# Four cross-attention layers on one core: pieces put ahead of a pair's scores, and the maxima subtracted one pair before the exponentials

## The chip, the core and the metric

The kernel runs on one core of one Trainium2 chip, in float32. Five engines work side by side, each through its own instructions in order: TensorE (PE in the profile; PEld is its weight load), VectorE (DVE), ScalarE (ACT), GpSimd (POOL), and SyncE (SP), which issues the DMAs. The metric is the device time of one execution in microseconds. Over three runs the kernel before took 4752.23 us (median; 4741.26 to 4752.79).

## The reference

`x` is [1, 2048, 256], the context [1, 1601, 512]. Four layers follow each other, each adding its output to `x`. Layers 0, 2 and 3 are "masked": 16 heads of 64, and a bias on four of the 1601 keys. Layer 1 is "grouped": an RMS norm, 16 heads of 16, four key heads, no mask.

```python
q = hidden_states @ Wq;  k = encoder_hidden_states @ Wk;  v = encoder_hidden_states @ Wv
logits = jnp.einsum('bhqd,bhkd->bhqk', q, k) * scale + col_bias
probs = jax.nn.softmax(logits, axis=-1)
out = jnp.einsum('bhqk,bhkd->bhqd', probs, v) @ Wo + bo + residual
```

## The kernel before

**Units and steps.** A masked layer is cut into 8 blocks of two heads (class `Masked`, L423) and 4 groups of 512 queries; one block with one group is a *unit* (class `Unit`, L682). The three masked layers have 96 units, the grouped one 16. A unit has 13 *steps*, one per 128 keys (the last has 65). The main loop (L1266) issues two steps at a time, a *pair*. Three phases of different units are in flight in a pair: at step t the scores of the unit with number t // 13, the exponentials of 18 steps back (NT + DELAY), and the values of 20 steps back (LAG 2, so the values of a pair use the exponentials of the pair before).

**One step of a masked unit.** `masked_scores` (L707): matmuls of keys with queries for both heads into a PSUM tile `s` [128, 2, 512] (L713), a ScalarE copy of `s` into an SBUF tile `p` (L725), and a VectorE maximum of `s` into the running `top` (L728, L730; none in step 0). `maxima` (L766), after the last step: eight transposes of `top` into another `s` tile (L773), a VectorE reduction to `ntop` (L774), and two DMAs that spread the row maxima over all partitions into `spread`. `maxima_spread` (L796): a ScalarE copy of `spread` into the PSUM tile `b` (L799). `subtract` (L802): `p <- p + b` on VectorE (L804). `masked_exp` (L806): the exponential in place on ScalarE (L809), and the running sum on GpSimd (L812, L814). `values` (L834): matmuls of `p` with `v` into `po` (L849); after the last step a copy to `oT` (L871).

**Pieces.** All other TensorE work is cut into pieces, which `Pieces` (L1069) hands out, at most one large one to a pair. *Fill pieces* (the list `fill`) are the key and value projections of the next block: `kT` (L459, copied by ScalarE in L460) and `v` (L413, L417), 14 for the four units of a block. *Due pieces* have a step of their own (`due`): the next unit's `queries` (L483, copied in L486) at step 11, `denominators` (transposes of `sums` in L887, reduction in L891) at step 8, `divide` (GpSimd, L912) and `project` (L920, added to `xs` in L932) at step 3. `own` runs what is due, `pair` adds a fill piece where nothing large was due. Fill pieces and queries write the PSUM tile `pm`, of which there is one. `denominators`, `project` and `maxima` write an `s` tile. **There are two `s` tiles** (pool `ps_s`, bufs=2), shared by these three and the scores; each covers two PSUM banks. Below these three are called *tile pieces* (the class argument `shared=False` marks the first two).

**Order.** TensorE, ScalarE and VectorE execute exactly in the order in which the Python code issues (the loop at L1321 chains each instruction to the one before on its engine). SyncE and GpSimd are ordered by the framework. In a pair of masked steps the order before is: subtract 0 and 1; scores 0 and 1 (matmuls, copy, maximum of each); exponentials 0 and 1; the copy of `spread`, where the next pair begins a unit; values 0 and 1; the pieces; `maxima`, where a unit's scores ended. So VectorE runs: subtract, subtract, maximum, maximum, and then whatever the piece leaves to it. ScalarE runs: copy, copy, exponential, exponential, and then the piece's copy.

Where a unit's values end in the first step of a pair (`ends`), its last values stand before the exponentials and the new unit's first values after the pieces.

The 22 `p` tiles (NP) are taken at the copy of the scores and come free when values and sum of the step are done, 20 steps later.

Of the kernel before, what the change touches and what calls it, by code (L numbers as in the profile page):

```python
# [32 lines left out]

@with_exitstack
def tile_cross_attention_stack(ctx: ExitStack, tc: tile.TileContext, t: dict, out: bass.AP):

# [29 lines left out]
    x, cond = t["x"], t["ctx_2048"]  # L68
# [8 lines left out]
    NT = len(TCH)  # L77
# [23 lines left out]
    class Scores:  # L101
# [16 lines left out]
        def pair(self, shape=(2, QB)):  # L118
            return self.pairs.tile([P, *shape], FP, name="s")
# [50 lines left out]
    def key_order(tok):  # L170
# [27 lines left out]
        first = const.tile([P, NTOK], FP, name="first")  # L198
        keep = small.tile([P, NTOK], FP, name="keep", bufs=1)
        nc.vector.tensor_tensor(pair, across(tok), along(tok), ALU.is_equal)  # L200
        nc.vector.tensor_tensor(pair, pair, before, ALU.mult)
        nc.vector.tensor_reduce(first, pair, AX.X, ALU.max)
        nc.vector.tensor_scalar(first, first, 0.0, None, ALU.is_equal)
        nc.vector.scalar_tensor_tensor(first, tok, 0.0, first, ALU.is_ge, ALU.mult)
# [18 lines left out]
        def sources(a, b):  # L223
            n = b - a
            wide = [P, n, NTOK]

            def tokens_of(v):
                return v.rearrange("p (o j) -> p o j", o=1).to_broadcast(wide)

            def at_positions(v):  # L230
                return v.rearrange("p (n o) -> p n o", o=1).to_broadcast(wide)

            test = probs.tile(wide, FP, name="p")
            spec = probs.tile([P, n], FP, name="p")
            place = probs.tile([P, n], FP, name="p")
            to, at = src[:, a:b], pos[:, a:b]
            nc.vector.tensor_tensor(test, at_positions(at), tokens_of(where), ALU.is_ge)
            nc.vector.tensor_reduce(to, test, AX.X, ALU.add)
            nc.vector.tensor_tensor(to, to, at, ALU.add)

            nc.vector.tensor_scalar(place, at, count, float(T), ALU.add, ALU.subtract)
            nc.vector.scalar_tensor_tensor(to, place, 0.0, to, ALU.is_lt, ALU.mult)
            nc.vector.tensor_tensor(test, at_positions(place), tokens_of(rank), ALU.is_equal)
            nc.vector.tensor_tensor(test, test, tokens_of(mine), ALU.mult)
            nc.vector.tensor_reduce(spec, test, AX.X, ALU.add)
            nc.vector.tensor_tensor(to, to, spec, ALU.add)
# [435 lines left out]
    class Unit:  # L682
# [119 lines left out]
        def subtract(self, c):  # L802
            m = TCH[c][1]
            nc.vector.tensor_tensor(self.p[c][:m], self.p[c][:m], self.less[:m], ALU.add)  # L804
# [205 lines left out]
    units = []  # L1010
# [4 lines left out]
    of = {}  # L1015
# [36 lines left out]
    def first_unit(i):  # L1052

        if i < NT / 2:
            first_block(i)
        if i == 1:
            layers[0].load_wo(made[0, 0])
            for b in range(NB):
                keep(0, b)
                pieces.at(2 * i + 2 + 2 * b, [(0, biases[b])])  # L1060
        if i == 3:
            token_marks(0)
        if i == 7:
            small_constants()
            for l in range(1, NL):
                token_marks(l)
            start_block(0)

    class Pieces:  # L1069
# [4 lines left out]
        def __init__(self):  # L1074
            self.fill, self.later = deque(), deque()
            self.due = {}
            self.credit = 0.0

        def at(self, step, found):
            for steps, piece in found:  # L1080
                self.due.setdefault(step + steps, []).append(piece)

        def own(self, steps):

            cost, taken = 0.0, False
            for step in steps:
                for piece in self.due.pop(step, ()):
                    piece.run()
                    cost += piece.cost
                    taken |= piece.shared and piece.cost > 0  # L1090
            return cost, taken

        def pair(self, steps, pairs):

            cost, taken = self.own(steps)
            many = len(self.fill) + len(self.later) > pairs
            while self.fill and not taken and (many or not cost):
                piece = self.fill.popleft()
                piece.run()
                cost += piece.cost  # L1100
                taken = piece.shared and piece.cost > 0

        def steps(self, steps, share):


            self.credit = max(min(self.credit + share, 2.5), -2.5)
            cost, taken = self.own(steps)
            self.credit -= cost
            while self.fill and not taken and self.credit >= self.fill[0].cost / 2:
                piece = self.fill.popleft()  # L1110
                piece.run()
                self.credit -= piece.cost
                taken = piece.shared and piece.cost > 0
# [13 lines left out]
    pieces = Pieces()  # L1127
# [53 lines left out]
    DELAY, LAG = 5, 2  # L1181
# [81 lines left out]
    def masked(unit):  # L1263
        return unit and unit.masked

    for first in range(0, N + NT + DELAY + LAG + 16, 2):  # L1266
        pair = [Step(first), Step(first + 1)]

        if any(masked(x.scoring) for x in pair):
            if psum.banks:  # L1270
                psum.by_pairs()
        elif pair[0].exping and not pair[0].exping.masked and not psum.banks:
            psum.singly()

        kn, cn = divmod(first + 2 - NT - DELAY, NT)
        ahead = of[kn] if cn == 0 and 0 <= kn < len(units) and of[kn].masked else None
        three = not ahead and not any(masked(x.exping) for x in pair)
        for x in pair:
            x.begin()
        for x in pair:  # L1280
            if masked(x.exping):
                if x.cb == 0 and x is pair[1]:
                    x.exping.maxima_spread()
                x.exping.subtract(x.cb)
        for x in pair:
            if masked(x.scoring):
                x.scoring.masked_scores(x.ca)

        ends = all(masked(x.valuing) for x in pair) and pair[0].cv == NT - 1
        if ends:  # L1290
            pair[0].valuing.values(NT - 1)
        for x in pair:
            if masked(x.exping):
                x.exping.masked_exp(x.cb)
        if ahead:
            ahead.maxima_spread()
        if not ends:
            for x in pair:
                if masked(x.valuing):
                    x.valuing.values(x.cv)  # L1300
        first_unit(first // 2)
        together = masked(pair[0].scoring) and (masked(pair[1].exping) or not pair[1].exping)
        for x in pair:
            x.grouped(three)
            x.end()
            if not together:
                pieces.steps([x.step], x.share())
        if together:
            pieces.pair([first, first + 1], round(pair[0].units_left() * NT / 2))
        if ends:  # L1310
            pair[1].valuing.values(0)
        for x in pair:
            if x.scoring and x.ca == NT - 1:
                x.scoring.maxima()
                if not x.scoring.masked:
                    pieces.at(first + 2, [(0, Piece(x.scoring.maxima_rows, 0.3))])


    last = {}
# [39 lines left out]
```

## Time and profile before

| | |
|---|---|
| median of three runs | 4752.23 us (4741.26 to 4752.79) |
| the profiled execution, its own time | 4745.24 us |
| its span, first to last instruction | 4743.5 us |
| TensorE busy | 4596.3 us, 97% |
| VectorE busy | 3744.2 us, 79% |
| ScalarE busy | 3226.5 us, 68% |
| GpSimd busy | 2977.4 us, 63% |
| mean granted TensorE clock | 0.992 |
| mean DMA traffic | 71 GB/s |

Busy time is per engine; a busy TensorE is one with matmuls in its pipeline, not one at its peak. An idle time stands with the instruction that followed it, and with what that instruction had waited for (the releaser). The chain of waits follows the end of the program back from releaser to releaser. L713 is line 713 of the kernel before. All times in what follows are in microseconds (us) from the start of the span, unless they are durations.

### The profile page before, as it was taken

The page shows a single profiled execution, that of the slowest core. Times are in us where ns is not written, and L with a number is a line of the kernel's source. Part 1 is how long each engine was busy: PE and PEld are TensorE (multiplying, and loading weights), DVE is VectorE, ACT ScalarE, POOL GpSimd, SP SyncE. Part 2 cuts the span into 40 slices and gives each one's busy share as a digit, 9 for nine tenths or more (in the row PEclk, how much of TensorE's full clock was granted, in tenths as well). Part 3 has the DMA queues.
Part 4 walks back from the last instruction along what each step waited for, and adds up shares of the span by engine and source line. Part 5 has one row for each costly group of instructions (what it writes and reads, how often), then busy time and mean ns, then how long its engine had stood idle before and what let it go on. Part 6 is the DMA issues. An engine that isn't in the chain of part 4 may idle for free.

```text
span 4743.5 us, 64047 instructions
## 1 busy us (share of the span) xinstructions
PE 4596.3 (97%) x23943; PEld 1914.1 (40%) x23943; DVE 3744.2 (79%) x3768; ACT 3226.5 (68%) x4013; POOL 2977.4 (63%) x1436
## 2 busy tenths in 40 slices
PE   8999999999989999999999999999999999999998
PEld 5444444444433333343444444344444444444433
DVE  5888888888876666653788888888888888888887
ACT  4777777777635555555677777777777777777776
POOL 3777777778730000000677777777777777777787
PEclk9999999999989999999999999999999999999999
DMA  4322323222201010021232232222232223232211
GB/s 150 85 84 79 88 77 86 81 80 78 74 27 38 20 29 21 20 61 39 79 89 84 78 89 78 84 80 82 76 91 73 86 81 85 75 86 77 84 36 39
DMA packets 349892, 337.63 MB, mean 71 GB/s; under 512 B 116421, under 2 KB 305381, under 8 KB 349580
## 3 DMA queue, kind: packets, MB, share of 16 engines
q1 hardware_dynamic: 346310, 328.14, 24.6%
q8 instruction: 189, 3.10, 0.3%
q0 software_dynamic: 1152, 3.28, 0.2%
q10 hardware_dynamic: 2118, 2.10, 0.1%
q14 instruction: 123, 1.01, 0.1%
HBM read 318.49 MB, written 14.69 MB: 70 GB/s over the span
## 4 chain that ended last, share of the span: by engine, by line
PE 87%; DVE 10%; issue 1%; ACT 1%; POOL 0%; DMA 0%; another core or an unknown queue 0%; ACTq 0%; DVEq 0%; POOLq 0%
PE po L849 28%; PE s L713 20%; PE t L744 9%; PE pm L413 7%; PE pm L459 6%; PE pm L483 4%; PE s L920 4%; DVE rden L891 2%; PE s L887 2%; DVE ntop L774 2%; DVE xs L932 2%; PE s L773 2%; DVE top L730 1%; DVE p L804 1%; PE t L819 1%
## 5 line engine op out<-in xcount | busy, mean ns | idle before, releaser
L814 POOL TENSOR_TENSOR sums<-sums,p 128x1024 f32<-128x1024 f32 x1145 | 2711.0, 2368 | 736.8 <-ACT p L809 566.0
L725 ACT COPY p<-s 128x1024 f32<-128x1024 f32 (+1 forms) x1248 | 1234.2, 1014 | 655.3 <-PE s L713 567.6
L804 DVE TENSOR_TENSOR p<-p,b 128x1024 f32<-128x1024 f32 (+1 forms) x1248 | 1461.2, 1210 | 55.5 <-ACT b L799 54.4
L849 PE MATMUL po<-p,v 128*64 128x512 f32 (+3 forms) x8320 | 1493.5, 522 | 4.9 <-ACT p L809 2.6
L730 DVE TENSOR_TENSOR top<-s,top 128x1024 f32<-128x1024 f32 (+1 forms) x1056 | 1291.4, 1223 | 234.1 <-ACT p L725 171.3
L713 PE MATMUL s<-q,kT 64*128 64x512 f32 (+1 forms) x4992 | 1336.7, 629 | 85.9 <-DVE ntop L774 23.2
L809 ACT ACTIVATE p<-p 128x1024 f32<-128x1024 f32 (+1 forms) x1248 | 1254.7, 1057 | 43.8 <-DVE p L804 42.6
L849 PEld LDWEIGHTS po<-p,v 128*64 128x64 f32 (+3 forms) x8320 | 365.7, 125 | 1115.8 <-issue 889.3
L713 PEld LDWEIGHTS s<-q,kT 64*128 64x128 f32 (+1 forms) x4992 | 388.6, 181 | 722.7 <-issue 215.5
L831 ACT ACTIVATE p<-t 128x512 f32<-128x512 f32 (+1 forms) x760 | 413.8, 594 | 297.6 <-PE t L819 256.5
L757 DVE TENSOR_REDUCE row_top<-t 128x1 f32<-128x512 f32 x700 | 451.2, 686 | 196.8 <-PE t L819 165.2
L912 POOL TENSOR_TENSOR oT<-oT,by 128x512 f32<-128x512 f32 x111 | 141.6, 1276 | 656.4 <-DMA by<-cols 336.1
L819 PE MATMUL t<-q,kT 32*128 32x512 f32 (+1 forms) x1520 | 489.1, 643 | 0.0
L744 PE MATMUL t<-kT,q 32*128 32x512 f32 (+1 forms) x1880 | 481.9, 553 | 0.0
L413 PEld LDWEIGHTS pm<-wv,ct 128*128 128x128 f32 (+1 forms) x2600 | 300.4, 187 | 130.4 <-issue 69.0
L413 PE MATMUL pm<-wv,ct 128*128 128x128 f32 (+2 forms) x2600 | 333.3, 281 | 1.7 <-ACT vs L417 0.7
L459 PE MATMUL pm<-ct,wk 128*128 128x256 f32 (+1 forms) x1344 | 316.7, 379 | 5.4 <-ACT ct L284 4.3
L774 DVE TENSOR_REDUCE ntop<-s 128x8 f32<-128x1024 f32 x96 | 117.6, 1225 | 228.4 <-PE s L773 228.4
L459 PEld LDWEIGHTS pm<-ct,wk 128*128 128x128 f32 x1344 | 232.2, 191 | 161.1 <-issue 99.3
L744 PEld LDWEIGHTS t<-kT,q 32*128 32x128 f32 x1880 | 182.5, 185 | 163.1 <-issue 96.7
L799 ACT COPY b<-spread 128x1024 f32<-128x1024 f32 x96 | 97.5, 1015 | 150.9 <-DVE p L804 150.0
L920 PE MATMUL s<-oT,wo 128*128 128x512 f32 x376 | 187.4, 621 | 2.8 <-DVE row_top L757 1.7
(176 smaller groups left out, 2249.8 us busy)
## 6 DMA issues: line engine op xcount, KB each, us to landing
ct<-ctxT SPq DMA_DIRECT2D x288, 512.0 KB
xT<-xT SPq DMA_DIRECT2D x100, 512.0 KB
spread<-cols SPq DMA_DIRECT2D x96, 512.0 KB
by<-cols SPq DMA_DIRECT2D x190, 128.0 KB
xT<-xs SPq DMA_DIRECT2D x16, 512.0 KB
ct<-ctxT SPq DMA_DIRECT2D x48, 130.0 KB
wk<-in_L_xattn_Wk_dram SPq DMA_DIRECT2D x24, 256.0 KB
wv<-in_L_xattn_Wv_dram SPq DMA_DIRECT2D x24, 256.0 KB
```

Of the source, the lines that this page charges most:

```text
L413: nc.tensor.matmul(pv[:md, d, :f], ct(k)[:, d * P : d * P + md], wv[:, k, :], start=(k == 0), stop=(k == NCT - 1),)
L459: nc.tensor.matmul(pk, u.wk[:, k, :], ct(k), start=(k == 0), stop=(k == NCT - 1))
L713: nc.tensor.matmul(s[:m, h, :], self.u.kT[r, a : a + m], self.q[r, :], start=True, stop=(a != TAIL),)
L725: nc.scalar.copy(p[:m], s[:m])
L730: nc.vector.tensor_tensor(self.top[:m], s[:m], self.top[:m], ALU.max)
L744: nc.tensor.matmul(s[:, at : at + n], self.q[r, ts(q, P)], self.u.kT[r, a : a + n], start=True, stop=True,)
L757: nc.vector.tensor_reduce(self.top[:, of, q, k : k + 1], s, AX.X, ALU.max)
L804: nc.vector.tensor_tensor(self.p[c][:m], self.p[c][:m], self.less[:m], ALU.add)
L809: nc.scalar.activation(p[:m], p[:m], AF.Exp)
L814: nc.gpsimd.tensor_tensor(self.sums[:m], self.sums[:m], p[:m], ALU.add)
L819: nc.tensor.matmul(s[:m], self.u.kT[r, a : a + m], self.q[r, :], start=True, stop=True)
L849: nc.tensor.matmul(to, v, p, start=(c == 0 and not part), stop=(c == NT - 1 and part != 0))
```

## The change

Three things move in pairs of masked steps; no computation is added or taken away.

1. *Pieces in front.* A new flag `pieces.scored` is set when a pair issued a tile piece. In the pair after that one (`front`), `pieces.pair` runs before the scores instead of at the end. If it ran something large, the end of that pair gets no piece.
2. *Subtractions one pair ahead.* The two subtractions that feed a pair's exponentials are issued in the pair before: that of its first step after the values and before the piece at the end, that of its second step as the very last thing, after `maxima`. The copy of `spread` goes with the first subtraction of a unit.
3. *Exponentials around the scores.* The first exponential of a pair is issued before its scores (behind the piece in front, if any), the second after them.

VectorE's order in a pair becomes: maximum, maximum, first subtraction for the next pair, what the piece at the end leaves to it, second subtraction. ScalarE's: the front piece's copy, exponential 0, copy, copy, exponential 1, the end piece's copy.

```diff
         def own(self, steps):
             cost, taken = 0.0, False
-            for step in steps:
-                for piece in self.due.pop(step, ()):
+            for step in sorted(step for step in self.due if step <= max(steps)):
+                for piece in self.due.pop(step):
                     piece.run()
                     cost += piece.cost
+                    self.scored |= piece.cost > 0 and not piece.shared
                     taken |= piece.shared and piece.cost > 0
             return cost, taken
...
+    def subtract(unit, c):
+        if c == 0:
+            unit.maxima_spread()
+        unit.subtract(c)
...
-        kn, cn = divmod(first + 2 - NT - DELAY, NT)
-        ahead = of[kn] if cn == 0 and 0 <= kn < len(units) and of[kn].masked else None
-        three = not ahead and not any(masked(x.exping) for x in pair)
+        ahead = []
+        for step in (first + 2, first + 3):
+            kn, cn = divmod(step - NT - DELAY, NT)
+            unit = of[kn] if 0 <= kn < len(units) else None
+            ahead.append((unit, cn) if masked(unit) else None)
+        three = not any(ahead) and not any(masked(x.exping) for x in pair)
         for x in pair:
             x.begin()
-        for x in pair:
-            if masked(x.exping):
-                if x.cb == 0 and x is pair[1]:
-                    x.exping.maxima_spread()
-                x.exping.subtract(x.cb)
+
+        together = masked(pair[0].scoring) and (masked(pair[1].exping) or not pair[1].exping)
+        steps, left = [first, first + 1], 0
+        if together:
+            left = round(pair[0].units_left() * NT / 2)
+        front = pieces.scored
+        pieces.scored = False
+        taken = pieces.pair(steps, left) if together and front else 0.0
+        if masked(pair[0].exping):
+            pair[0].exping.masked_exp(pair[0].cb)
         for x in pair:
             if masked(x.scoring):
                 x.scoring.masked_scores(x.ca)
...
-        for x in pair:
-            if masked(x.exping):
-                x.exping.masked_exp(x.cb)
-        if ahead:
-            ahead.maxima_spread()
+        if masked(pair[1].exping):
+            pair[1].exping.masked_exp(pair[1].cb)
         if not ends:
             for x in pair:
                 if masked(x.valuing):
                     x.valuing.values(x.cv)
         first_unit(first // 2)
-        together = masked(pair[0].scoring) and (masked(pair[1].exping) or not pair[1].exping)
+        if ahead[0]:
+            subtract(*ahead[0])
...
-        if together:
-            pieces.pair([first, first + 1], round(pair[0].units_left() * NT / 2))
+        if together and not taken:
+            pieces.pair(steps, left)
         if ends:
             pair[1].valuing.values(0)
         for x in pair:
             if x.scoring and x.ca == NT - 1:
                 x.scoring.maxima()
+                pieces.scored |= x.scoring.masked
...
+        if ahead[1]:
+            subtract(*ahead[1])
```

More of the change, by code (lines that the diff above doesn't have):

```diff
@@ L1077, in __init__ @@
             self.credit = 0.0
+            self.scored = False
         def at(self, step, found):
@@ L1101, in pair @@
                 taken = piece.shared and piece.cost > 0
+            return cost
         def steps(self, steps, share):
```

## The prediction

> **What bounds the kernel now.** I read the page's busy times and its chain by engine first.
>
> ```profile
> PE 4596.3 (97%) x23943; PEld 1914.1 (40%) x23943; DVE 3744.2 (79%) x3768; ACT 3226.5 (68%) x4013; POOL 2977.4 (63%) x1436
> ...
> PE 87%; DVE 10%; issue 1%; ACT 1%; POOL 0%; DMA 0%; another core or an unknown queue 0%; ACTq 0%; DVEq 0%; POOLq 0%
> ```
>
> TensorE sets the end, save for 10% of the chain that lies on VectorE. Where that is, the chain of waits in the middle of the last layers shows (start, us, what):
>
> ```profile
> 3043.80 1.93 PE s L920 x4
> 3045.73 0.02 issue
> 3045.75 1.24 DVE xs L932
> 3046.99 0.04 issue
> 3047.03 1.13 PE s L713 x4
> 3048.16 1.87 PE po L849 x8
> 3050.03 1.92 PE pm L459 x8
> 3051.95 1.92 PE s L713 x8
> 3053.87 1.87 PE po L849 x8
> ```
>
> After a tile piece (here `project`) one of the two `s` tiles is full. The second scores of the next pair wait for VectorE to empty it. From the end of the piece to the start of the values it takes 48.16 - 45.73 = 2.43, where an undisturbed pair takes 1.92: 0.51 lost. The waits by releaser name three kinds of such tiles, near 96 times each:
>
> ```profile
> PEld s L713 <- DVE ntop L774: 99.7, 93, 1.1
> PEld s L713 <- DVE rden L891: 98.2, 91, 1.1
> PEld s L713 <- DVE xs L932: 87.9, 81, 1.1
> ```
>
> Two units are 13 pairs, a cycle; busy times for one (span, PE, PEld, DVE, ACT, POOL):
>
> ```profile
> 3019.50:3097.30 77.80, 76.26 (x343) 32.40 (x341) 65.89 (x59) 56.75 (x66) 61.22 (x28) 1.00 0.29 82
> ```
>
> A cycle has six tile pieces: 6 x 0.51 = 3.06 of its 77.8 is all that putting pieces in front can win. VectorE is 85% busy here. Last, one undisturbed pair in the timeline:
>
> ```profile
> 3015.29 2.34 DVE L804 TENSOR_TENSOR p<-p,b 128x1024 f32<-128x1024 f32 x2
> 3015.70 1.99 PE L713 MATMUL s<-q,kT 64*128 64x512 f32 x8
> ...
> 3016.93 1.93 ACT L725 COPY p<-s 128x1024 f32<-128x1024 f32 x2 [1.30 <-PE s L713]
> 3017.62 1.94 PE L849 MATMUL po<-p,v 128*64 128x512 f32 x8
> 3017.98 2.56 DVE L730 TENSOR_TENSOR top<-s,top 128x1024 f32<-128x1024 f32 x2 [0.35 <-ACT p L725]
> ...
> 3018.74 2.02 ACT L809 ACTIVATE p<-p 128x1024 f32<-128x1024 f32 x2
> ```
>
> The maximum does not start with its scores: it starts 0.04 after the *copy* of the same tile (3016.93 + 1.01). The subtractions run before the scores are there, so nothing waits for them.
>
> **What the skill says.** The Trainium skill, "PSUM — Partial Sum Buffer", section "PSUM bank collisions raise a hardware error": the compiler's scheduler puts a dependency between any two instructions on different engines that touch the same bank, two readers too. The trace agrees: the 0.35 idle above; so I hold copy, then maximum, for an order that the change can't loosen. "Perfetto Trace Analysis", section "Tensor Engine Instruction (MATMUL, LD_WEIGHTS)": VectorE and ScalarE are strict FIFO, and TensorE's end times are modelled. The former is what the code's chained order shows; for the latter I take distances in the chain, not TensorE's busy time. The same page's "Optimization Strategy" reads a gap that repeats as a sign of too few buffers; here 0.26 of idle in front of L713, and two `s` tiles.
>
> **The change, part by part.** *Pieces in front.* After a tile piece, a piece of 1.92 covers VectorE's 1.24: the 0.51 goes. What is late next: nothing follows the pair's values, so the next pair's scores come at once. *Subtractions.* The same 26 per cycle, moved from ahead of the maxima to behind them. The spread copies keep their place on ScalarE almost to the instruction. *Exponential 0* moves ahead of the copies. This makes a ring that was not there before: maxima of a pair, subtraction 0 for the next pair, exponential 0, copy 0, maximum 0 and 1 of that pair. Queued behind the waiting exponential on ScalarE are both copies; for them waits VectorE's maximum, and for this the `s` tile that the next tile piece needs.
>
> Steps, from back-to-back rows: maxima 1.22 + 1.33 (2.55); from their start to the next operation 2.46; a subtraction ends 1.21 after its start; exponential 1.05; the copy behind it 0.93; kT copy 0.37; hand-over 0.04. The ring: (2.46 + 1.21 - 2.55 = 1.13) + 0.04 + 1.05 + 0.93 + 0.04 + 2.55 = 5.74 a pair. TensorE's pair with one piece is 1.92 + 1.87 + 1.92 = 5.71. So the ring is no shorter than TensorE's own work, and what it once loses it doesn't win back.
>
> Follow a front pair C and the next, D, from the end of C's front piece (0):
>
> - ScalarE: kT copy 0.04 to 0.41, exponential 0 to 1.4, copy 0 to 2.34 (its scores were ready at 1.13).
> - VectorE: maxima of C 2.38 to 4.93; subtraction 0 for D to 6.05.
> - TensorE: scores and values of C to 3.79; D's first scores to 4.75; the second must wait for the second maximum, 4.98, and with refilling the array (the group after an idle takes 1.13, not 0.96) end at 6.04; values of D to 7.91. Lost so far 0.33.
> - ScalarE: exponential 0 of D 6.09 to 7.15, copy 0 to 8.08 (its scores lay ready at 4.95). VectorE: maximum 0 of D 8.12 to 9.34.
> - If D ends in a tile piece, it needs the tile of D's first scores: it starts at 9.39 instead of 7.91, with refilling 1.63 lost.
>
> If D ends in a fill piece, it runs 7.91 to 9.83 and hides this lag, but the lag stays: pair E's maximum 0 ends at 9.34 + 5.74 = 15.08, its values at 9.83 + 3.79 = 13.62, and E's tile piece loses 1.51 + 0.15 = 1.66.
>
> Over a cycle, numbering pairs from 0 at the start of a unit that begins a pair, tile pieces end pairs 1 (project), 4 (denominators), 6 (maxima), 8, 10, 12 (maxima), and fronts are 0, 2, 5, 7, 9, 11. Losses: behind each front 6 x 0.33 = 1.98; pairs 1, 8 and 10 at 1.63 = 4.89; pair 4 1.66; pair 12, where the queries run first and the transposes need the second maximum (10.67 against 9.83), 0.89 + 0.15 = 1.04; pair 6 none, since a fill piece precedes its transposes. Sum 9.57, less the 3.06 that is saved: **+6.5 per cycle**.
>
> Scores and masked exponentials overlap in 30.6 units of layer 0 (13 x 32 - 18 steps) and 62.6 of layers 2 and 3: 46.6 cycles. The last two have no fill pieces (a cycle there takes 74.0 already, VectorE 65.9); the ring alone is 13 x 5.74 = 74.6 and six reductions that push subtraction 1 make some +3 each. 44.6 x 6.5 + 2 x 3 = 296. The profiled execution's own 4745 plus 296 is 5041; that execution lay 7 below the median shown, so I say **5045**.
>
> At nothing I put: the wider `due` search (issue order only). DMAs: queries in front free their buffer, and so issue the next xT load, some 3.8 earlier, fill pieces the next context load likewise; both are prefetches. `denominators` and `maxima` issue their small DMAs on SP later by their stall, up to 1.7; `divide` comes three steps later and `project` eight, some 8 and 23 away, the spread two pairs; that slack hides it, and without it a late spread would hold subtraction 0 and so the ring, one for one. GpSimd (61 of 78) follows the exponentials. The grouped layer (PE 868 of 880) keeps its order but for the 18 steps at each border.
>
> **Unknown sizes.** Not shown is how the ring's members overlap when they alternate across engines. With isolated means (1.21 + 1.06 + 1.01 + 2 x 1.22, four hand-overs) it is 5.87, and each tile piece, two rings on, loses up to 0.2 more: +8.5 per cycle, 5141. With every step 3% shorter it is 5.57: some 0.25 less per event, +5, 4978.
>
> **Rivals.**
> 1. *The maximum needs no copy* (faster). Were maximum 0 of D free to follow its scores, VectorE would run maxima and subtractions alone, 4.7 a pair (5.9 with a reduction), finish maximum 0 of D near 7.15, and the tile piece at 7.58 would find its tile free: all of 3.06 won, 44.6 x 3.06 = 136, 4609. It decides at 1.45 of the 1.96 lost per event: less lost than 0.51, and the change gains. For it: the maxima's values need only `s`. Against it: 0.35 behind the copy, 203 such idles in the trace of `top`. 9%.
> 2. *The wait only changes place*: tile pieces lose about the 0.51 that scores lose now. 4745 within 14. It wants a ring shorter by 1.45; the rows leave no such room. 3%.
> 3. *The lag is partly caught up*: steps 0 have no maximum (1.2 of relief per unit), and stalls of TensorE let the ring gain. At a quarter to a third of the losses kept beyond the gain, +1 to +3 per cycle: 4790 to 4880. 8%.
> 4. *Also the `p` tiles run short*: copies already wait 42.9 for sums on GpSimd (34 times). Later exponentials make later sums; three times that on top of the upper bound is beyond 5140. 5%.
>
> That the change doesn't take effect I rule out: the flag is set by every tile piece.
>
> **How the numbers follow.** Forecast 75%, then 9, 3, 8, 5. The range 4870 to 5140 holds most of the forecast and the top of the third rival. About 0.3% (14) is what a measurement can tell from no change. Faster 0.10, same 0.03, slower 0.87.
>
> **What would show it.** Right: the waits of L713 for ntop, rden and xs fall to a fraction, and TensorE's idle before `project` and `denominators` grows to 1 to 1.5 each, released by the maximum of `top`; ScalarE idles 1 to 2 before exponential 0, released by the subtraction (now 42.6 in all, then several hundred); a cycle takes 83 to 86; VectorE's and ScalarE's shares of the chain rise at TensorE's cost. Wrong: a cycle under 77, maxima that start while the copy of their tile runs, or tile pieces that start right behind the values.

## The result

The change made the kernel slower: 4953.85 us against 4752.51 (medians of four runs each), a ratio of 1.0429 with a 95% interval of 1.0411 to 1.0447. The forecast was 5045 with a range of 4870 to 5140. So the sign was right, and the loss is two thirds of what was worked out: 205.6 us in the profiled executions (spans 4949.1 and 4743.5) instead of some 300.

The page of the changed kernel, busy times and the chain by engine:

```profile
PE 4562.2 (92%) x23943; PEld 1919.9 (39%) x23943; DVE 3754.8 (76%) x3768; ACT 3186.8 (64%) x4013; POOL 2981.9 (60%) x1436
...
PE 60%; DVE 17%; ACT 13%; issue 7%; DMA 1%; POOL 1%; ACTq 0%; DVEq 0%; SPq 0%; POOLq 0%
```

The chain has moved from TensorE (87% before) to a round trip: 17% on VectorE, 13% on ScalarE, which had 1%, and 7% in which the engine waited for nothing that the profile shows ("issue"). The shares alone don't tell a loss: with pieces in front alone, which is faster than the kernel before, the three engines have 63%, 23% and 7%. The waits by releaser (total, times, longest; lines are two further down than before, so L715 are the scores, L732 the maximum, L727 the copy, L806 the subtraction, L811 the exponential, L922 `project`, L889 `denominators`):

```profile
ACT p L811 <- DVE p L806: 590.8, 347, 8.9
DVE top L732 <- ACT p L727: 507.3, 484, 9.4
...
PE s L922 <- DVE top L732: 124.6, 88, 1.5
...
PE s L889 <- DVE top L732: 100.5, 89, 1.5
```

ScalarE's wait for the subtractions is 590.8 where it was 42.6, and the two tile pieces wait 1.4 and 1.1 us each for a maximum, a wait that the kernel before did not have. What was to go is mostly gone. Call *eviction* the VectorE operation that empties the tile of a tile piece: `xs` for `project`, `ntop` for `maxima`, `rden` for `denominators`. The waits of the scores' weight loads for `xs` and `ntop` were 87.9 and 99.7, and are 9.4 and 6.1. That for `rden` fell only from 98.2 to 70.0; where the matmuls themselves wait for it, as at 3014.64 in the timeline (0.39), the front piece was the short one of 65 keys, which takes 0.93 and not 1.8.

One turn of the new ring, in the timeline behind a front pair (start, us, what, and in brackets the idle before it):

```profile
3004.06 2.55 DVE L732 TENSOR_TENSOR top<-s,top 128x1024 f32<-128x1024 f32 x2 [0.66 <-ACT p L727]
...
3005.48 2.32 PE L715 MATMUL s<-q,kT 64*128 64x512 f32 x8
...
3006.53 2.34 DVE L806 TENSOR_TENSOR p<-p,b 128x1024 f32<-128x1024 f32 x2
3007.73 1.94 PE L851 MATMUL po<-p,v 128*64 128x512 f32 x8
3007.78 1.06 ACT L811 ACTIVATE p<-p 128x1024 f32<-128x1024 f32 x1 [1.40 <-DVE p L806]
3008.74 1.91 ACT L727 COPY p<-s 128x1024 f32<-128x1024 f32 x2
...
3009.77 2.55 DVE L732 TENSOR_TENSOR top<-s,top 128x1024 f32<-128x1024 f32 x2 [0.89 <-ACT p L727]
```

From maxima to maxima it takes 3009.77 - 3004.06 = 5.71. The scores that the copy at 3008.74 reads had started at 3005.48. The next thing on TensorE is `denominators`, at 3011.14, after 1.47 of idle: it needed the tile of the first maximum, which ended at about 3011.0.

A cycle of 13 pairs, from one `denominators` to the same place 13 pairs on:

```profile
3011.14:3093.17 82.03, 75.32 (x365) 33.53 (x365) 66.11 (x59) 55.73 (x66) 61.34 (x29) 1.00 0.29 79
```

82.03 against 77.8: +4.2 a cycle. Over the 44.6 cycles with fill pieces this is 189 of the 205.6 us; the last two, without fill pieces, take 77.84 and 77.85 instead of 75.34 and 73.78 (from `rden` to `rden`), 6.6 more. The prediction had named 83 to 86 for a cycle as a sign that it is right; that sign did not come, 82.0 lies below it.

### The profile page after: what moved, and what is told of

It is laid out like the page before. It is cut to its first block, busy times and chain, and to the rows that moved or that the text cites. A ratio compares the mean times of both kernels' runs of the same rounds, so it can differ in the third digit from the quotient of the medians.

```text
span 4949.1 us, 64074 instructions
## 1 busy us (share of the span) xinstructions
PE 4562.2 (92%) x23943; PEld 1919.9 (39%) x23943; DVE 3754.8 (76%) x3768; ACT 3186.8 (64%) x4013; POOL 2981.9 (60%) x1436
## 4 chain that ended last, share of the span: by engine, by line
PE 60%; DVE 17%; ACT 13%; issue 7%; DMA 1%; POOL 1%; ACTq 0%; DVEq 0%; SPq 0%; POOLq 0%
PE s L715 16%; PE po L851 13%; DVE top L732 13%; ACT p L727 10%; PE t L746 8%; PE pm L415 5%; PE pm L461 4%; PE s L922 4%; ACT p L811 2%; PE s L775 2%; PE pm L485 2%; DVE p L806 1%; PE s L889 1%; DVE rden L893 1%; DVE top L730 1%
## 5 line engine op out<-in xcount | busy, mean ns | idle before, releaser
L732 DVE TENSOR_TENSOR top<-s,top 128x1024 f32<-128x1024 f32 (+1 forms) x1056 | 1292.4, 1224 | 563.1 <-ACT p L727 507.3
L811 ACT ACTIVATE p<-p 128x1024 f32<-128x1024 f32 (+1 forms) x1248 | 1326.4, 1063 | 592.6 <-DVE p L806 590.8
L806 DVE TENSOR_TENSOR p<-p,b 128x1024 f32<-128x1024 f32 (+1 forms) x1248 | 1479.2, 1208 | 19.5 <-ACT b L801 18.4
L715 PE MATMUL s<-q,kT 64*128 64x512 f32 (+1 forms) x4992 | 1311.8, 627 | 42.0 <-DVE rden L893 18.0
L727 ACT COPY p<-s 128x1024 f32<-128x1024 f32 (+1 forms) x1248 | 1197.0, 1007 | 53.8 <-PE s L715 50.6
L715 PEld LDWEIGHTS s<-q,kT 64*128 64x128 f32 (+1 forms) x4992 | 399.6, 182 | 780.9 <-DVE top L732 348.0
L461 PE MATMUL pm<-ct,wk 128*128 128x256 f32 (+1 forms) x1344 | 305.6, 371 | 3.5 <-issue 2.8
L922 PE MATMUL s<-oT,wo 128*128 128x512 f32 x376 | 186.2, 618 | 130.0 <-DVE top L732 124.6
L730 DVE TENSOR_TENSOR top<-s,p 128x1024 f32<-128x1024 f32 x96 | 117.5, 1224 | 210.9 <-ACT p L727 210.8
L419 ACT COPY v<-pm 128x256 f32<-128x256 f32 (+1 forms) x168 | 60.1, 357 | 241.3 <-PE pm L415 239.5
```

The costliest lines, as they stand in the source:

```text
L461: nc.tensor.matmul(pk, u.wk[:, k, :], ct(k), start=(k == 0), stop=(k == NCT - 1))
L715: nc.tensor.matmul(s[:m, h, :], self.u.kT[r, a : a + m], self.q[r, :], start=True, stop=(a != TAIL),)
L727: nc.scalar.copy(p[:m], s[:m])
L732: nc.vector.tensor_tensor(self.top[:m], s[:m], self.top[:m], ALU.max)
L811: nc.scalar.activation(p[:m], p[:m], AF.Exp)
```

## Experiments

The change has three parts: F, pieces in front; S, the subtractions a pair ahead; E, exponential 0 ahead of the score copies (which needs S). The theory on record is that of the ring (subtraction 0, exponential 0, copy 0, maxima). Rivals lay the loss on F or on S alone. The first four runs take the parts singly and two at a time; the kernel before that ran beside them took 4748.61. Each ratio is to the kernel before that ran beside it, with its 95% interval; it can differ by some 0.1% from the quotient of the medians.

### F and S without E

```diff
-        if masked(pair[0].exping):
-            pair[0].exping.masked_exp(pair[0].cb)
         for x in pair:
             if masked(x.scoring):
                 x.scoring.masked_scores(x.ca)
...
+        if masked(pair[0].exping):
+            pair[0].exping.masked_exp(pair[0].cb)
         if masked(pair[1].exping):
             pair[1].exping.masked_exp(pair[1].cb)
```

> The change, with exponential 0 issued behind the two score copies again (pieces in front and early subtractions stay). Ring theory (subtraction 0, exponential 0, copy 0, maximum 0 and 1, each waiting for the last, is what costs): with the exponential behind the copies the copies follow their scores, the ring is open, and the 0.5 us behind each tile piece is won at least in part: 4690 to 4745, no idle of TensorE in front of project and denominators. Rival A (pieces in front cost: the pair behind a front pair comes too early for two s tiles): the front pieces are all still there, so 4880 or more. Rival B (the new place of the subtractions on VectorE costs): likewise 4880 or more.

Measured: 4680.32 us, ratio 0.9856 (0.9836 to 0.9876), **faster than both kernels**, and better than expected. Moving one exponential per pair behind two copies is worth 274 us (272 by the ratios, since the two ran beside different runs of the kernel before). Its waits:

```profile
ACT p L811 <- DVE p L806: 51.8, 11, 8.6
...
PE s L922 <- DVE top L732: 35.2, 88, 0.5
...
PE s L889 <- DVE top L732: 22.4, 48, 0.5
```

ScalarE's wait is back at 51.8, and a tile piece waits 0.4 to 0.5 instead of 1.4. A cycle from one `ntop` to the same place 13 pairs on takes 3088.11 - 3011.97 = 76.14, so E adds 82.03 - 76.14 = 5.89 to it, 274 over 46.6 cycles. Both rivals fall as causes by themselves: all of F and S is in this kernel. Not every new wait is E's, though. Here too the tile piece of a pair behind a front pair waits up to 0.49, and the second scores there take 0.24 longer; those belong to the pieces in front, and F alone shows them too (third run).

### S and E without F

```diff
-        front = pieces.scored
+        front = False
```

> The change without pieces in front (early subtractions and exponential 0 ahead of the copies stay). Ring theory: the ring of 5.7 us is still closed, and every pair that is longer on VectorE (an eviction between the subtractions) lags behind it: slower than before by some 3 us per 13 pairs, 4860 to 4930; the front pieces account for the rest of the 200 us, because what a front pair costs the ring is not won back. Rival A (pieces in front cost): 4740 to 4770. Rival B (place of the subtractions): about the changed kernel's 4954, less at most 50.

Measured: 4858.55, ratio 1.0242 (1.0219 to 1.0265). The number lies just under what the ring theory expected, but the next run but one shows that the reason given was wrong: it is not the ring that costs here. The ring is closed, and ScalarE waits in it:

```profile
DVE top L732 <- ACT p L727: 493.7, 394, 9.4
ACT p L811 <- DVE p L806: 386.5, 280, 8.2
```

A cycle takes 80.15 here (`rden` at 2994.54 and 3074.69), 6.17 a pair, which is longer than the ring's 5.71.

### F alone

The subtractions and both exponentials stand as in the kernel before; the flag and the call in front are kept.

```diff
+        front = pieces.scored
+        pieces.scored = False
+        taken = pieces.pair(steps, left) if together and front else 0.0
...
-        if together:
-            pieces.pair([first, first + 1], round(pair[0].units_left() * NT / 2))
+        if together and not taken:
+            pieces.pair(steps, left)
```

> The kernel before with pieces in front alone (subtractions and exponentials where they were). Ring theory: no ring; the wait of the second scores for the eviction is hidden by the front piece, but the pair behind a front pair comes early and waits some for VectorE's maxima: 4700 to 4752. Rival A (pieces in front cost by themselves): 4800 or more. Rival B: 4610 to 4700, all of the 3 us per 13 pairs won.

Measured: 4717.46, ratio 0.994 (0.992 to 0.996). F by itself gains 31 us, a fifth of the 3.06 per cycle that it removes. The tile pieces now wait 0.4 to 0.5 for the maxima (35.2 in 88 waits of `project`, 23.2 in 48 of `denominators`), and the second scores behind a front pair wait for a maximum too:

```profile
PE s L715 <- DVE top L732: 57.7, 187, 2.2
PE s L922 <- DVE top L732: 35.2, 88, 0.5
PE s L889 <- DVE top L732: 23.2, 48, 0.5
```

### S alone

Without F (as in the second run) and without E (as in the first).

> The kernel before with early subtractions alone (no pieces in front, both exponentials behind the copies). Ring theory: no ring, but each eviction now stands behind subtraction 0 on VectorE and comes some 0.3 us later, six times per 13 pairs: 4760 to 4850. Rival A (pieces in front): same as before, 4740 to 4765. Rival B (place of the subtractions is the whole cause): 4900 or more.

Measured: 4863.98, ratio 1.0241 (1.0219 to 1.0262), just above the expected range. The early subtraction costs 115 us where no piece stands in front. Its waits show how:

```profile
PE s L715 <- DVE rden L893: 96.7, 91, 1.1
PE s L715 <- DVE xs L934: 77.9, 81, 2.0
PE s L715 <- DVE ntop L776: 23.2, 90, 0.3
```

In the kernel before, the second scores stood idle 0.26 for each of the three. Now it is 1.06 for `rden` and 0.96 for `xs`, and 0.26 still for `ntop`. Subtraction 0 stands ahead of the first two evictions on VectorE, and it waits for the maxima itself; I had put the delay at 0.3. Where the next pair begins a unit, it waits for the copy of `spread` too, which stands behind both exponentials (3034.81 in the chain; the second scores at 3038.24 then idle 1.65). In the chain of waits a turn without that copy reads, one after the other:

```profile
3047.89 1.21 DVE p L806
3049.10 1.15 DVE rden L893
3050.25 0.04 issue
3050.29 1.13 PE s L715 x4
```

The table of the parts (each ratio to the kernel before that ran beside it):

| parts | us | ratio |
|---|---|---|
| none | 4748.61 | 1 |
| F | 4717.46 | 0.994 |
| S | 4863.98 | 1.0241 |
| S, E | 4858.55 | 1.0242 |
| F, S | 4680.32 | 0.9856 |
| F, S, E (the change) | 4953.85 | 1.0429 |

E adds nothing to S without F, and 274 with F. S costs 115 without F and gains 37 with it. So the ring shows no loss without front pieces. That was measured only on top of what S costs there, where a pair takes 6.17 on average and leaves the ring room; E can't be run without S, so what the ring would cost at the old pace is not shown. It costs together with front pieces, behind which the next pair comes after 3.8 instead of 5.7.

The next four runs look into the loss of E with F (the kernel before beside them: 4754.06).

### The maximum ahead of the copy

In the changed kernel, the order of the two readers of a score tile is turned round.

```diff
-            nc.scalar.copy(p[:m], s[:m])
             if c == 1:
                 self.top = work.tile([P, 2, QB], FP, name="top", bufs=1)
                 nc.vector.tensor_tensor(self.top, s, self.p[0], ALU.max)
             elif c:
                 nc.vector.tensor_tensor(self.top[:m], s[:m], self.top[:m], ALU.max)
+            nc.scalar.copy(p[:m], s[:m])
```

> The changed kernel with the maximum of a score tile issued before its copy, so that the copy waits for the maximum and not the other way round. Ring theory: maximum 0 of the pair behind a front pair follows its scores instead of subtraction 0, exponential 0 and copy 0; the tile comes free at the end of copy 0, 1.3 us sooner, and VectorE is no longer in the ring: most of the 200 us back, 4740 to 4800. Rival (ScalarE's order alone costs, whatever the maximum waits for: the copies stand behind exponential 0 as before): 4920 or more.

Measured: 4862.41, ratio 1.0227 (1.021 to 1.0244). The number fell between the theories: 91 us back, not 150 to 210. `project` waits 0.40 now, for a copy, where it waited 1.4 for a maximum; but the copies wait for maxima in turn:

```profile
PE s L922 <- ACT p L732: 34.5, 87, 0.7
...
ACT p L732 <- DVE top L731: 648.0, 985, 4.4
```

The chain of this kernel also lies on GpSimd for 10% (1% in the changed kernel), and its subtractions wait 151.2 for the copy of `spread` (18.4 there); what these two cost stays open. A later run gives the price of this order in the kernel before.

### Exponential 0 ahead of the front piece

```diff
+        if masked(pair[0].exping):
+            pair[0].exping.masked_exp(pair[0].cb)
         taken = pieces.pair(steps, left) if together and front else 0.0
-        if masked(pair[0].exping):
-            pair[0].exping.masked_exp(pair[0].cb)
```

> The changed kernel with exponential 0 ahead of the front piece, not behind it: on ScalarE it runs while TensorE works on the front piece. Theory 1 (the ring starts late in the front pair, because exponential 0 waits there for the front piece and its ScalarE copy; it is 1 us of ScalarE behind the piece's end): the front pair's copy 0 starts some 0.3 us sooner (it then waits for its scores), six times per 13 pairs, so 0.3 x 6 x 44.6 = 80 us come back: 4850 to 4900. Theory 2 (exponential 0 behind the front piece is the whole loss): 4680 to 4760. Theory 3 (the pair behind the front pair alone decides): 4930 to 4960.

Measured: 4924.03, ratio 1.0359 (1.0342 to 1.0376): 30 us better than the change, nearest to the third theory. That the exponential of a *front* pair waits for the piece's copy is at most a small part. What it wins there it pays in part elsewhere: ScalarE's waits for the subtractions rise from 590.8 (347 times) to 858.6 (521 times). It is the pair *behind* the front pair whose exponential comes late.

### Exponential 0 between the copies

```diff
-        if masked(pair[0].exping):
-            pair[0].exping.masked_exp(pair[0].cb)
         for x in pair:
             if masked(x.scoring):
                 x.scoring.masked_scores(x.ca)
+            if x is pair[0] and masked(x.exping):
+                x.exping.masked_exp(x.cb)
```

> The changed kernel with exponential 0 between the two score copies. Ring theory: copy 0 and maximum 0 leave the ring; what is left is subtraction 0, exponential 0, copy 1, maximum 1, 4.4 us, shorter than TensorE's 5.7 a pair, and the tile of maximum 0 is free for the next tile piece: 4690 to 4790. Rival (an exponential ahead of any copy costs the same): half to all of the loss stays, 4850 to 4950.

Measured: 4818.54, ratio 1.0137 (1.012 to 1.0154): half of E's 274, outside the expected range. The tile pieces have what was expected of them, 0.48 of wait, as with both exponentials behind. But the second scores wait more often:

```profile
PE s L715 <- DVE top L732: 78.9, 185, 2.2
PE s L922 <- DVE top L732: 42.6, 88, 0.5
PE s L715 <- DVE top L730: 21.7, 43, 0.8
PE s L889 <- DVE top L732: 21.6, 45, 0.5
```

That is 228 waits of 0.44. In the front pair, copy 1 stands behind the exponential there, so maximum 1 ends 0.4 later by the steps of the prediction (copy 1 to 4.05 instead of 3.27, maximum 1 to 5.31 instead of 4.93), and the next pair's second scores need it. The trace has it so: a front piece ends at about 3083.65, and the next pair's second scores start at 3088.97, 5.32 later. I had looked at maximum 0 alone.

### Both subtractions behind the piece

On top of F and S, subtraction 0 moves behind the piece at the end, and with it the copy of `spread` that goes with a unit's first subtraction. It still stands ahead of `maxima`.

```diff
-        if ahead[0]:
-            subtract(*ahead[0])
...
         if together and not taken:
             pieces.pair(steps, left)
+        if ahead[0]:
+            subtract(*ahead[0])
```

> Pieces in front, both exponentials behind the copies (the fastest kernel so far, 4680), and now both subtractions behind the piece at the end and its eviction. If subtraction 0 gains there because it fills the time in which VectorE waits for the tile piece, this falls back to the kernel with pieces in front alone, 4705 to 4730. If the gain came from the eviction's or the exponentials' place, it stays at 4670 to 4690.

Measured: 4721.36, ratio 0.9938 (0.9921 to 0.9954), the same as F alone. So the 37 us that S adds to F come from the place of subtraction 0 (or of the copy that goes with it, which this run does not part from it). The waits fit the first: ahead of the eviction of `project` VectorE idles 77.3 us here (83 times) and 15.2 (3 times) where subtraction 0 comes first, so it runs while VectorE would wait for the tile piece.

### Two more: the price of the reversed order, and another ring

The kernel before beside these two took 4739.35. First, the kernel before with the maximum ahead of the copy, the same edit as above.

> The kernel before with the maximum of a score tile ahead of its copy, and nothing else: what the reversed order costs by itself. In the run on the changed kernel it gave back only half of the 200 us. If its own price is the reason (copies, and with them the next scores, wait for VectorE, where the two subtractions come first), the kernel before becomes slower with it, 4850 to 5150. If the reversed order is free here (4740 to 4770), half of the changed kernel's loss does not run through the wait of the maximum for the copy.

Measured: 5262.85, ratio 1.1089 (1.106 to 1.1118), more than expected. The order that opens the ring costs over 500 us where there is no ring: ScalarE waits for maxima, which stand behind two subtractions, and TensorE for the copies (134.8 in 273 waits) and for the copy of the queries (149.1 in 89), which ScalarE does later. The granted clock was 0.975 in this run and 0.992 in the kernel before, and what part of the loss goes with that is not shown.

```profile
ACT p L730 <- DVE top L729: 938.9, 880, 6.1
```

So the 91 us that it *gains* on the changed kernel may be a net of a larger gain and such a price. That is not shown: there the subtractions stand behind the maxima, and how large each part is the two runs don't say.

Second, F and S with subtraction 1 in its own pair:

```diff
+        if masked(pair[1].exping):
+            subtract(pair[1].exping, pair[1].cb)
         if masked(pair[0].exping):
             pair[0].exping.masked_exp(pair[0].cb)
...
-        if ahead[1]:
-            subtract(*ahead[1])
```

> The fastest kernel so far (pieces in front, early subtractions, both exponentials behind the copies; 4680), with subtraction 1 moved into its own pair, behind the maxima. Ring theory: this closes another ring of the same members, maxima, subtraction 1, exponential 1, copy 0 of the next pair, 5.7 us a pair without the piece's copy, and the loss is back: 4900 or more. Rival (what counts is that VectorE is free for the maxima when the scores come, which subtraction 1 ahead of them prevents for 1.1 us in the pair behind a front pair): 4620 to 4690.

Measured: 5272.07, ratio 1.1114 (1.1084 to 1.1143). Sign and waits are those of a ring:

```profile
ACT p L811 <- DVE p L806: 973.1, 615, 8.5
...
DVE top L732 <- ACT p L727: 643.6, 580, 17.3
```

The size is not explained by it alone: the chain of this kernel also runs through the small DMAs of `denominators` and the division (in a stretch of 30 us, 18% of it on the two DMAs), and the granted clock was 0.978. I have not separated them.

## Why the prediction was right, and where it was off

**The mechanism** was that of the prediction, at its places. By the timeline, seen from the end of the front piece (3001.78): exponential 0 of the next pair starts at 6.00 (predicted 6.09), the pair's maximum 0 starts at 7.99 (8.12), the tile piece at 9.36 (9.39). The ring takes 5.71 (5.74). The first rival (the maximum needs no copy) is refuted by 580 idles of `top` behind a copy, 719.9 in all. The fourth (the `p` tiles run short) did not come: the copies' waits for sums on GpSimd went from 42.9 (34 times) to 0.2 (once). The late spread that was put at nothing stayed there: subtractions wait 18.4 for its copy, 54.4 before.

**The sum** was 9.57 of new losses per cycle, less 3.06; measured is 7.42 less 3.18 for the measured cycle, each taken as the distance from start to start over that of an undisturbed one. The pairs are numbered as in the prediction:

| term, us per cycle | predicted | measured |
|---|---|---|
| second scores behind a front piece | 1.98 | 1.97 |
| tile pieces: pairs 1, 8, 10 | 4.89 | 4.54 |
| pair 4 | 1.66 | 0.86 |
| pair 12 | 1.04 | 0.73 |
| copy of `po` behind the ring | - | 0.47 |
| pieces next to each other | - | -1.15 |

1. *The 0.15 after an idle.* I added it to each tile piece that starts after an idle and called it refilling the array. No such lengthening is there; the piece is shorter instead: `project` takes 1.79 from its start to the next (1.92 before), `denominators` 1.04 (1.16), and a full front piece behind it 1.81 to 1.88 (1.91 to 1.98). Over a cycle this is 5 x 0.15 that isn't there and 1.15 that is gained: 1.9 of the 2.15 by which the new losses were too large.
2. *Pair 4.* Its tile piece starts 15.06 after the front piece's end, where 15.13 was predicted; the ring was right. TensorE had come later, though: in pair 3 the values of the new unit wait 0.40 for the copy of `po` to `oT`, which stands on ScalarE behind the ring. That copy I had left out of the walk. What it costs (0.47) it takes from the stall.
3. *Second scores.* The sum is as predicted by chance, its parts are not: three times the 0.33 (pairs 3, 8, 10), one of 0.31 in pair 6, none in pairs 1 and 12, and one of 0.67, which is the wait for `rden` behind the short front piece. The working names 1.13 for the group after an idle, as the chain shows it; its 6.04 takes the 1.06 from start to start, which is the one to take.
4. *Pair 1.* Its tile piece starts 8.94 after the front piece's end, where pairs 8 and 10 take 9.36: step 0 has no maximum, which was the third rival's relief. It is 0.42, of which 0.33 shows as the missing loss of the second scores and the rest as 1.39 of idle instead of 1.47.

**"It once loses, it doesn't win back"** was the right reading of two nearly equal lengths, but the prediction did not say what follows from it: that the ring shows no cost without front pieces, which by themselves gain 31, and only together with them the 274. I expected the ring to cost some 3 per cycle without front pieces (second run); it adds nothing there, and the 110 measured belong to **subtraction 0 ahead of the eviction**. This term I had at nothing ("the same 26 per cycle, moved"), and with front pieces it costs nothing: the front piece covers the eviction. The cover should have been named, with what lies under it: 115 us. That the forecast did not suffer from this omission was luck.

The two outer sizes of the prediction (5141 and 4978) multiply by 46.6 cycles, where its middle takes 44.6 and twice 3; worked out alike they are 5130 and 4974.

The best order found keeps two parts of the change, F and S, and puts the exponential back behind the copies: 4680.32, 68 us below the kernel before.

## What to carry to other kernels

When a step is moved ahead on an engine that works in the order of issue, follow what then stands behind it, once round, until the chain meets itself. Compare the length of that ring with the pace of the bounding engine, and ask where it loses time that it can't win back. An early issue helps only if its input is there: here that of the exponential was there in the front pairs; in the pairs behind them it was not, and the exponential held two copies, and with them the tiles. Of a change in parts that touch the same queue, measure the parts in pairs: each of F, S and E has another sign or size next to another.

## What was not expected of the hardware

Two pieces of full 128-row matmuls next to each other on TensorE take some 0.1 us less each than where each stands between scores and values, which use half of the rows or columns. In the changed kernel `project` starts at 3036.10, the fill piece behind it at 3037.89 and the scores at 3039.77: 1.79 and 1.88, where the kernel before has 1.92 and 1.98. It needs no idle: in the kernel with F and S, eight transposes that directly follow the values and precede the queries take 1.07 from start to start (1.16 before). From these runs I can give the number, not the cause.
